# The last layer's scan: separate PSUM rings for the experts, and a scheduling priority for the scan's own work

## The chip, the cores and the metric

The kernel runs on one core of a Trainium2 chip, as one launch. The metric is the device time of one execution in microseconds; the number for a kernel is the median over its runs. The profile is one execution, recorded by the hardware profiler.

## The reference

An input of 4 sequences of 1024 tokens with 128 features passes four layers, each an attention-like part and a feed-forward part, with a residual and a layer norm after each. All is float32. What matters here is the last layer and the feed-forward part ahead of it:

```
# L2_ffn: 8 experts, the best 2 for each token (sparse)
h = silu(gate) * up;  y = h @ w2;  out = sum of the 2 chosen, weighted

# L3_attn: a selective state-space recurrence, 256 channels, 16 states
x = rmsnorm(resid); skip = x @ skip_w.T; xs = silu(conv1d(x @ in_w.T))
delta = softplus(xs @ wd1.T @ wd2.T + b); Bm = xs @ wb.T; Cm = xs @ wc.T
h[t] = exp(delta[t] * A) * h[t-1] + delta[t] * xs[t] * Bm[t]
y[t] = sum over states of h[t] * Cm[t]
out  = resid + ((y + xs * W_D) * silu(skip)) @ out_w.T

# L3_ffn: 8 experts, all computed for every token, gated by top-p 0.8
h = relu(x @ W1 + b1);  y = h @ W2 + b2;  out = sum over e of gate * y
```

## The kernel before

Every step is recorded in a Python program of generators; a scheduler then gives each engine its own list of instructions. It takes an instruction that is ready by its model of time, and among ready ones that with the lowest priority number, which is its place in the recorded program unless something else is said. On the chip each engine works its list strictly in that order, and semaphores make it wait for what it needs. Tiles come from pools; a pool of n buffers makes the writer of the next tile wait until the readers of an older one are done.

The last stage (`l3`, L1595) works on 8 halves of 512 tokens (4 sequences, 2 halves each). For each half:

- *Preparation* (`l3_prepare`, L1715): norm, transpose `pt`, input projection `pxe`, convolution and SiLU on VectorE, projection `pdb`, softplus of `pd0` and `pd1` with a chain of ScalarE and VectorE operations that keeps both in PSUM, and a write of the rows of B and C to DRAM (`rows`, L1786).
- *Scan* (`l3_scan`, L1816): 16 steps, one for each state. A step loads two broadcast rows, `bn` and `cn` (L1841, SyncE's queue, four buffers), multiplies on GpSimd (`db`, L1846), computes `da` on ScalarE (L1850) and scans on VectorE (L1851), both for two groups of 128 channels, and multiplies on GpSimd again (`hc`, L1862, four buffers). From the second sequence on an accumulating DMA adds every second `hc` to the one before (L1867). TensorE sums the `hc` in PSUM by identity products (`pys`, L1833).
- *End*: the last sums and the gate (`l3_sum`, L1876), then output product `po`, norm, transpose, router `prl` and gates `gt` (`l3_finish`, L1901).
- *Last experts* (`l3_ffn_head`, L1941, and `l3_ffn`, L1959): a head (`pgt`, `pb2`), then 8 experts, so 64 in all. An expert loads its weights `wh` (L1674, three buffers), computes four tiles `ph` (one bank each) with a ReLU on ScalarE (`hh`, L1977), one tile `py` of 16 products (one bank), and adds it to `h_acc` by four VectorE instructions (L1993).

The loop of `l3` weaves these: at each step of one half's scan it also takes one step of the end of the half before, one of the preparation of the next half, one or two of the sparse experts of the layer before (`moe`: tiles `ph` from `xgT`, `py` from `mh`, weights `wx`), and three or four of the last experts (`work`). A half's experts may begin when its end is more than three steps old (`age`).

PSUM has 8 banks of 512 float32 for each partition. During the scan `banks(y0=1, y1=1, da=2, ff=4)` (L1680) gives one bank to each sum, two to `da`, and four, as one ring `ff`, to everything else: preparation, ends, sparse experts and last experts. When all scans are recorded, `l3_experts` (L1639) closes these pools and opens one ring of eight (L1658) for what is left of the last experts.

Of the kernel before, what the change touches and what calls it, by code (L numbers as in the profile page):

```python
# [40 lines left out]
E3, NST, DDELTA, KCONV = 256, 16, 64, 4  # L41
# [17 lines left out]
class Net:  # L59
# [1535 lines left out]
    def l3(self, moe, fp):  # L1595

        c3 = self.c3  # L1600
        halves = [dict(b=b, h=h) for b in range(B) for h in range(2)]
        for i, u in enumerate(halves):
            u["prev"] = halves[i - 1] if u["h"] else None
        halves[0] = dict(self.c3["first"], **{k: halves[0][k] for k in ("prev",)})
        for i, u in enumerate(halves[1:], 1):
            u["prev"] = halves[i - 1] if u["h"] else None
        work = self.l3_experts(fp)
        end = iter(())
        for i, u in enumerate(halves):
            nxt = iter(())  # L1610
            if i + 1 < len(halves):
                if halves[i + 1]["h"] == 0:
                    while "done" not in self.m2["st"][halves[i + 1]["b"]]:
                        next(moe)
                nxt = self.l3_prepare(halves[i + 1])
            u["final"] = i + 1 == len(halves)
            for n, f in enumerate(self.l3_scan(u)):
                next(end, None)
                next(nxt, None)
                for k in range(1):  # L1620
                    next(self.m2["rest"], None)
                next(moe, None)
                if i == 0:
                    for k in range(1):
                        next(moe, None)
                for k in range(4 if n % 8 == 7 else 3):
                    next(work)
                for v in c3["todo"]:
                    v["age"] += 1
            for f in chain(end, nxt):  # L1630
                pass
            end = chain(self.l3_sum(u), self.l3_finish(u))
        for f in end:
            next(work)
        c3["all"] = True
        for f in work:
            pass

    def l3_experts(self, fp):  # L1639


        c3 = self.c3
        heads, self.wh = [], {}

        def others():

            while len(heads) < 2 and c3["todo"] and ("all" in c3 or c3["todo"][0]["age"] > 3):
                heads.append((c3["todo"].pop(0), []))
            return heads[1:]

        i = 0
        while True:
            others()
            if "all" in c3 and c3["banks"]:

                c3["banks"].close()
                c3["banks"] = None
                c3["ctx"].enter_context(self.banks(ff=8))  # L1658
            if heads:
                u = heads[0]  # L1660
                if not u[1]:
                    yield from self.l3_ffn_head(*u, fp)
                yield from self.l3_ffn(*u, i, fp, others)
                heads.pop(0)
                i += NE
            elif "all" in c3:
                return
            else:
                yield
# [6 lines left out]
    def l3_pools(self, ctx):  # L1676
        tc = self.tc
        sp = ctx.enter_context(tc.tile_pool(name="ssm", bufs=1))
        wp = ctx.enter_context(tc.tile_pool(name="ssm2", bufs=2))
        banks = ctx.enter_context(self.banks(y0=1, y1=1, da=2, ff=4))  # L1680
        self.mtags = dict(t="ff", h=("ff",), o="ff")
        self.c3.update(sp=sp, wp=wp, ctx=ctx, banks=banks)

# [257 lines left out]
    def l3_ffn_head(self, u, head, wp):  # L1941

        nc, c3, h = self.nc, self.c3, u["h"]
        ff = lambda s, n: self.psb("ff", s, n)
        acc = wp.tile([P, 4, D], F32, name="h_acc")
        head.append(acc)
        pg = ff([NE, 4, P], "pgt")
        for c in range(4):
            self.tr(pg[:, c, :], u["gt"][:, c, :])
        gT = wp.tile([NE, 4, P], F32, name="gT", bufs=1)  # L1950
        nc.scalar.copy(gT, pg)
        yield
        pb = ff([P, 4, D], "pb2")
        for c in range(4):
            self.mm(pb[:, c, :], gT[:, c, :], c3["b2"])
        nc.vector.tensor_add(acc, pb, self.xN[u["b"]][:, 4 * h : 4 * h + 4, :])
        yield

    def l3_ffn(self, u, head, i0, wp, others):  # L1959

        nc, c3, b, h, gt, acc = self.nc, self.c3, u["b"], u["h"], u["gt"], head[0]
        ff = lambda s, n: self.psb("ff", s, n)
        NK = F3 // P
        x = self.xT[b][:, h * 512 : h * 512 + 512]
        ahead = None
        for e in range(NE):
            if i0 + e == 0:
                for k in range(2):
                    self.l3_weights(k, wp)
            self.l3_weights(i0 + e + 2, wp)  # L1970
            w = self.wh.pop(i0 + e)
            hs = []
            for k in range(NK):
                ph = ff([P, 512], "ph")
                self.mm(ph, w[:, k * P : (k + 1) * P], x)
                ht = wp.tile([P, 512], F32, name="hh", bufs=6)
                nc.scalar.activation(ht, ph, AF.Relu, bias=self.col("h_b1", i=e * NK + k))  # L1977
                hs.append(ht)
                yield
            py = ff([P, 4, D], "py")  # L1980
            for c in range(4):
                for k in range(NK):
                    self.mm(
                        py[:, c, :],
                        hs[k][:, c * P : (c + 1) * P],
                        w[:, F3 + k * D : F3 + (k + 1) * D],
                        k == 0,
                        k == NK - 1,
                    )
                if c == 1:  # L1990
                    yield
            for c in range(4):
                nc.vector.scalar_tensor_tensor(  # L1993
                    acc[:, c, :],
                    py[:, c, :],
                    gt[:, c, e : e + 1],
                    acc[:, c, :],
                    ALU.mult,
                    ALU.add,
                )  # L2000
            yield

            if e >= NE - 3:
                if ahead is None and others():
                    ahead = self.l3_ffn_head(*others()[0], wp)
                if ahead is not None:
                    next(ahead, None)
        for f in ahead or ():
            pass
        self.norm(wp, acc, b, 4 * h, 4, last=True, ps=ff, act=True)  # L2010

# [193 lines left out]
```

## Time and profile before

| what | value |
|---|---|
| time, median of 3 runs | 2294.14 us (2287.42 to 2300.56) |
| profiled execution: time and span | 2289.61 us and 2287.8 us |
| TensorE busy over the span | 1974.5 us (86%) |
| VectorE, ScalarE, GpSimd busy | 1351.7 us (59%), 1207.2 us (53%), 1023.3 us (45%) |
| first product of the recurrence on GpSimd | at 1386 us |
| first `ph` of the last experts | at 1545 us |
| `po` of the last half | from 2176 us |
| GpSimd products `hc` and `db` | 128 of 2463 ns and 112 of 2593 ns in their largest groups |

In the profile's rows PE is TensorE's products, PEld its weight loads, DVE is VectorE, ACT ScalarE, POOL GpSimd, SP SyncE; a letter q behind an engine is its queue. Each row of a list of waits names the engine, tile and line that waited, then who released it, then the total in us, how often, and the longest. A float32 product of 128x128 by 512 columns is recorded as two matmul instructions. A line of the code can be that of a helper (L127 holds nearly all products), so tiles are told apart by name. Granted clock (PEclk) is the share of TensorE's full clock.

### The profile page before, as it was taken

How to read it: one execution, taken by the hardware profiler on the slowest of the kernel's cores; microseconds unless marked ns; L12 is line 12 of the kernel's file. 1: busy time of each engine (PE TensorE's matmuls, PEld its weight loads, DVE VectorE, ACT ScalarE, POOL GpSimd, SP SyncE). 2: the span in 40 equal slices, each digit the busy share in tenths (PEclk: the TensorE clock that was granted, in tenths of full speed). 3: DMA queues.
4: the chain of work that ended last, by engine and by line, in shares of the span. 5: the costliest groups of instructions: out<-in, count | busy, mean ns of one | idle time of the engine just before them, and what ended most of it. 6: DMA issues, size and time to landing. Idle time of an engine off the chain costs nothing.

```text
span 2287.8 us, 46393 instructions
## 1 busy us (share of the span) xinstructions
PE 1974.5 (86%) x17806; PEld 1382.2 (60%) x17806; DVE 1351.7 (59%) x3693; ACT 1207.2 (53%) x2621; POOL 1023.3 (45%) x812
## 2 busy tenths in 40 slices
PE   6667979879999999999989876589888989898998
PEld 3455655444477777787767664346555656565666
DVE  7457743424355565665555556686777787877521
ACT  6543443332244444444555456476767786767443
POOL 5100230000023235224243429988789979888500
PEclk9757989979999999999999987799999999999999
DMA  3000110005000010031223147456776666676421
GB/s 107 0 15 23 30 39 1 19 10 174 1 3 2 3 35 15 17 91 46 76 70 88 32 142 231 127 182 196 202 204 178 177 169 192 175 208 178 122 60 51
DMA packets 138558, 211.10 MB, mean 92 GB/s; under 512 B 18597, under 2 KB 75936, under 8 KB 137952
## 3 DMA queue, kind: packets, MB, share of 16 engines
q1 hardware_dynamic: 126192, 173.87, 24.7%
q0 software_dynamic: 12144, 34.26, 7.1%
q8 instruction: 140, 2.29, 0.4%
q14 instruction: 82, 0.67, 0.1%
HBM read 160.29 MB, written 23.16 MB: 80 GB/s over the span
## 4 chain that ended last, share of the span: by engine, by line
PE 40%; DVE 13%; ACT 11%; issue 4%; DMA 2%; POOL 1%; SPq 0%; ACTq 0%; DVEq 0%; POOLq 0%
PE py L127 7%; PE ph L127 6%; PE po L1126 5%; DVE db L1851 5%; PE pqk L127 4%; PE pa_m L127 4%; PE kp_mo L127 3%; PE pr L1196 2%; PE pv L127 2%; PE pys L127 2%; ACT hh L1977 2%; ACT da L1850 1%; PE pt L131 1%; PE kp_mo L131 1%; ACT xN L174 1%
## 5 line engine op out<-in xcount | busy, mean ns | idle before, releaser
L1059 POOL TENSOR_TENSOR qt<-r_q,sb_c_turn 128x256 f32<-128x256 f32 (+1 forms) x256 | 164.0, 661 | 448.5 <-ACT r_q L1051 442.9
L1862 POOL TENSOR_TENSOR hc<-db,cn 128x1024 f32<-128x1024 f32 x128 | 312.9, 2463 | 63.5 <-PE pys L127 27.1
L127 PEld LDWEIGHTS py<-wh,hh 128*128 128x128 f32 x2048 | 248.6, 193 | 85.6 <-issue 36.1
L1846 POOL TENSOR_TENSOR db<-ud,bn 128x1024 f32<-128x1024 f32 x112 | 284.1, 2593 | 12.7 <-DMA wh<-in_wH 6.2
L127 PE MATMUL py<-wh,hh 128*128 128x128 f32 x2048 | 257.1, 278 | 22.9 <-ACT hh L1977 12.5
L127 PE MATMUL ph<-xT,wh 128*128 128x512 f32 x512 | 250.3, 606 | 16.8 <-ACT hh L1977 5.9
L1977 ACT ACTIVATE hh<-ph,sb_cols 128x512 f32<-128x512 f32 x256 | 170.6, 681 | 131.9 <-PE ph L127 105.5
L1117 DVE TENSOR_TENSOR a<-pa_m,sb_c_near 128x256 f32<-128x256 f32 x256 | 96.7, 420 | 202.6 <-PE pa_m L127 202.6
L1074 ACT ACTIVATE kN<-kp_mo,sb_c_trig 128x128 f32<-128x128 f32 x448 | 130.2, 372 | 132.0 <-PE kp_mo L131 122.2
L1850 ACT ACTIVATE da<-dl,aneg 128x512 f32<-128x512 f32 x224 | 153.1, 689 | 77.8 <-DVE db L1851 76.6
L127 PE MATMUL pys<-hc,sb_c_ident 128*128 128x512 f32 x324 | 159.7, 621 | 29.3 <-POOL hc L1862 21.3
L1851 DVE TENSOR_TENSOR_SCAN db<-da,carry,db 128x512 f32<-128x512 f32 x128 | 158.0, 1268 | 21.1 <-POOL db L1846 11.9
L1851 DVE TENSOR_TENSOR_SCAN db<-da,db 128x512 f32<-128x512 f32 x128 | 149.6, 1207 | 9.5 <-POOL db L1846 6.0
L127 PEld LDWEIGHTS ph<-xT,wh 128*128 128x128 f32 x512 | 89.8, 194 | 98.1 <-issue 57.1
L1993 DVE SCALAR_TENSOR_TENSOR h_acc<-py,gt,h_acc 128x128 f32<-128x128 f32 x256 | 71.8, 343 | 124.6 <-PE py L127 124.0
L127 PE MATMUL pqk<-xT,wE 128*128 128x256 f32 x512 | 136.8, 390 | 8.2 <-ACT coT L1193 4.2
L127 PEld LDWEIGHTS pys<-hc,sb_c_ident 128*128 128x128 f32 x324 | 61.0, 199 | 96.7 <-issue 60.6
L729 POOL DMA_INDIRECT orows<-o,ix x20 | 18.9, 944 | 186.6 <-DVE o L727 160.4
L127 PEld LDWEIGHTS pqk<-xT,wE 128*128 128x128 f32 x512 | 89.0, 194 | 22.0 <-DVE cv L1036 8.1
L131 PE MATMUL pt<-sb_c_ident,xN 128*128 128x128 f32 x224 | 54.4, 343 | 51.4 <-ACT xN L174 32.2
L1193 ACT COPY coT<-pt 128x512 f32<-128x512 f32 x64 | 37.6, 587 | 116.1 <-PE pt L131 116.1
L127 PE MATMUL po<-ht,wD 128*128 128x512 f32 x192 | 94.3, 598 | 0.0
(456 smaller groups left out, 4340.2 us busy)
## 6 DMA issues: line engine op xcount, KB each, us to landing
wx<-in_wF SPq DMA_DIRECT2D x92, 384.0 KB, 3.3
bn<-rows SPq DMA_DIRECT2D x128, 256.0 KB, 5.0
cn<-rows SPq DMA_DIRECT2D x128, 256.0 KB, 4.3
wh<-in_wH SPq DMA_DIRECT2D x64, 512.0 KB, 4.1
hc<-hc POOLq DMA_DIRECT2D x47, 512.0 KB, 6.6
xrows<-zero SPq DMA_DIRECT2D x4, 1472.0 KB, 11.9
xg<-xrows SPq DMA_DIRECT2D x20, 256.0 KB, 3.0
yrows<-ys SPq DMA_DIRECT2D x20, 256.0 KB, 3.3
```

The costliest lines, as they stand in the source:

```text
L127: return self.nc.tensor.matmul(out=out, lhsT=lhsT, rhs=rhs, start=start, stop=stop)
L131: self.nc.tensor.transpose(out, in_, self.ident[0:n, 0:n])
L1059: nc.gpsimd.tensor_mul(u["qt"][:, m, a:], u["q"][:, a:], c2["turn"][:, m, o + a : o + 2 * P])
L1074: self.nc.scalar.activation(u["kN"][:, c, m, :], pk[:, c, :], AF.Copy, scale=trig[:, k, m : m + 1])
L1117: nc.vector.tensor_mul(u["a"][:, i, :, :], pa[i], self.c2["near"][:, None, :].to_broadcast([P, 2, P]),)
L1126: self.nc.tensor.matmul(out=u["po"][self.HALF[j], i, c, :], lhsT=lhsT, rhs=rhs, start=key not in u["begun"], stop=True, skip_group_check=True,
L1846: nc.gpsimd.tensor_mul(db, ud, bc[0])
L1850: nc.scalar.activation(da, dl[:, ec, :], AF.Exp, scale=aneg[:, j : j + 1])
L1851: nc.vector.tensor_tensor_scan(db[:, ec, :], da, db[:, ec, :], carry[:, ec, n : n + 1] if h else 0.0, ALU.mult, ALU.add,)
L1862: nc.gpsimd.tensor_mul(hc, db, bc[1])
L1977: nc.scalar.activation(ht, ph, AF.Relu, bias=self.col("h_b1", i=e * NK + k))
L1993: nc.vector.scalar_tensor_tensor(acc[:, c, :], py[:, c, :], gt[:, c, e : e + 1], acc[:, c, :], ALU.mult, ALU.add,)
```

## The change

It has three parts.

1. The ring `ff` of four banks becomes two rings of two during the scan: `ff` for preparation, ends and sparse experts, `ex` for the last experts and their heads. The last norm of an expert's half keeps `ff`.
2. When all scans are recorded, the ring of eight becomes `ff=2, ex=6`.
3. One step of the scan, one of the end of the half before and one of the preparation of the next are recorded inside `high_priority(offset=1000)`: in the scheduler they count as if recorded 1000 instructions earlier. Sparse experts and last experts keep their place. A scan's generator is now stepped 16 times by a counter, and is run out (it has nothing left to record) ahead of the rest of the end and the preparation, which stand outside of the priority.

```diff
             u["final"] = i + 1 == len(halves)
-            for n, f in enumerate(self.l3_scan(u)):
-                next(end, None)
-                next(nxt, None)
+            scan = self.l3_scan(u)
+            for n in range(NST):
+                with self.tc.high_priority(offset=1000):
+                    next(scan)
+                    next(end, None)
+                    next(nxt, None)
                 for k in range(1):
                     next(self.m2["rest"], None)
                 next(moe, None)
...
-            for f in chain(end, nxt):
+            for f in chain(scan, end, nxt):
                 pass
             end = chain(self.l3_sum(u), self.l3_finish(u))
...
-                c3["ctx"].enter_context(self.banks(ff=8))
+                c3["ctx"].enter_context(self.banks(ff=2, ex=6))
...
-        banks = ctx.enter_context(self.banks(y0=1, y1=1, da=2, ff=4))
+        banks = ctx.enter_context(self.banks(y0=1, y1=1, da=2, ff=2, ex=2))
         self.mtags = dict(t="ff", h=("ff",), o="ff")
...
     def l3_ffn_head(self, u, head, wp):
-        ff = lambda s, n: self.psb("ff", s, n)
+        ff = lambda s, n: self.psb("ex", s, n)
...
     def l3_ffn(self, u, head, i0, wp, others):
-        ff = lambda s, n: self.psb("ff", s, n)
+        ff = lambda s, n: self.psb("ex", s, n)
...
-        self.norm(wp, acc, b, 4 * h, 4, last=True, ps=ff, act=True)
+        self.norm(wp, acc, b, 4 * h, 4, last=True, ps=self.bank("ff"), act=True)
```

The built program of the changed kernel has the same instructions of work on every engine; ScalarE's table loads are 112 instead of 110. What differs is their order from about the first sparse experts beside the recurrence on.

## The prediction

> **What bounds the kernel now.** The change touches only the last stage, so I first asked the table of stretches for its three phases: the recurrence alone, the recurrence with the last experts beside it, the last experts alone.
>
> ```profile
> core 0: us, PE busy (x) PEld busy (x) DVE busy (x) ACT busy (x) POOL busy (x), PEclk, DMA share, GB/s
> 1380.00:1540.00 160.00, 110.83 (x416) 66.15 (x417) 117.74 (x185) 96.11 (x200) 150.44 (x75) 0.84 0.54 169
> 1540.00:2150.00 610.00, 551.04 (x2752) 361.55 (x2751) 455.22 (x871) 436.94 (x792) 529.55 (x276) 0.98 0.68 187
> 2150.00:2288.00 138.00, 123.32 (x688) 88.14 (x686) 33.40 (x120) 56.52 (x92) 0.00 (x0) 0.97 0.19 56
> ```
>
> Up to 1540 us POOL is the limit: 150.4 of 160 us busy with the recurrence's products. From there on TensorE (PE) is: 551 of 610 us beside the recurrence, 123 of 138 after it, and its work is the same before and after the change. So the end moves by what PE's idle time changes, and there are 610 - 551 = 59 us of it between 1540 and 2150. POOL has 80 us free there. The list of waits says what PE idles for (engine and line that waited, releaser: total us, times, longest):
>
> ```profile
> PE py L127 <- ACT hh L1977: 12.4, 15, 1.8
> PE pys L127 <- DMA hc<-hc: 7.8, 4, 3.0
> PE ph L127 <- ACT hh L1977: 6.8, 5, 2.9
> ...
> PE psk L127 <- ACT hh L1977: 3.7, 3, 2.2
> ...
> PE ph L127 <- DVE h_acc L1993: 2.2, 3, 1.0
> ```
>
> The four rows with hh or h_acc are waits for an expert's activation or for a PSUM bank: 12.4 + 6.8 + 3.7 + 2.2 = 25 us. The other 34 us are spread over sums of the recurrence, preparation, norms and the sparse experts. The same list for POOL shows what the priority could free:
>
> ```profile
> POOL hc L1862 <- PE pys L127: 27.1, 11, 9.1
> POOL hc L1862 <- DVE db L1851: 10.1, 7, 3.3
> ```
>
> Last, the timeline of experts alone, with eight banks (start, duration, engine, line, out<-in; in brackets the idle time before):
>
> ```profile
> 2254.44 1.13 DVE L1993 SCALAR_TENSOR_TENSOR h_acc<-py,gt,h_acc 128x128 f32<-128x128 f32 x4 [5.88 <-PE py L127]
> ...
> 2254.68 3.60 PE L127 MATMUL ph<-xT,wh 128*128 128x512 f32 x8
> ...
> 2255.80 0.69 ACT L1977 ACTIVATE hh<-ph,sb_cols 128x512 f32<-128x512 f32 x1 [0.71 <-PE ph L127]
> ...
> 2258.12 3.73 PE L127 MATMUL py<-wh,hh 128*128 128x128 f32 x32
> ...
> 2261.69 3.60 PE L127 MATMUL ph<-xT,wh 128*128 128x512 f32 x8
> ```
>
> An expert is four ph (8 instructions, 2254.68 to 2258.12, so 0.86 us each) and one py (32 instructions, 3.57 us): 7.01 us, back to back, because the ph of one expert stand ahead of the py of the expert before.
>
> **The change, part by part.** All counts of order below are from the built program of the changed kernel: where its instructions stand on each engine.
>
> *Two rings of two.* Experts are numbered from 1 to 64. With two banks a ph needs the bank of the ph two before it, and the second ph of an expert needs the bank of the last py. Built, no ph of experts 9 to 48 stands ahead of the end of the previous py (before: 28 of 160 do). What such an expert costs when ACT and VectorE (DVE) are free, from the timeline: h_acc ends at 2255.57, 0.89 us after the first ph starts. An activation ends 0.95 us after its ph's slot (0.26 until 2255.80, then 0.69). For the hand-over back to PE I take 0.06 us, from a relu of 0.67 us that starts at 1979.82 and the ph that it releases at 1980.55. First ph 0 to 0.86; second 0.95 to 1.81 (lost 0.09); third waits for the first's activation, 1.87 to 2.73 (0.06); fourth 2.82 to 3.68 (0.09); py starts at 3.74 (0.06), runs three products (0.33) and stands until the fourth activation at 4.69 (0.62); 3.24 us more end it at 7.93. That is **0.92 us lost per expert**.
>
> - Experts 49 to 56 run after the recurrence and before the new pools: 8 x 0.92 = **+7 us**.
> - Experts 1 to 48 run beside it. The gap inside py: 30 of 40 experts (9 to 48) have nothing else there, so 48 x 0.75 x 0.62 = 22 us. The gap before the second ph: 28 of 40 have other work in it, mostly sums of 1.72 us, which hide it. The other 30%, 14 experts, meet a DVE that is 75% busy (455 of 610) with scans of 1.2 us; an h_acc behind one is 0.75 x 1.2 = 0.9 us late: 14 x 1.0 = 14 us. The three gaps before third ph, fourth ph and py are open in about 105 of 144 cases; ACT is 72% busy with operations of 0.69 us, a delay of 0.5 us, and 105 x 0.57 = 60 us. After one such stall the next activation is no longer late, so I take half, 30. Sum 66 us, against the 25 us of such waits today: **+41 us**. Upper end, no halving: +71. Lower end, the isolation from the recurrence's long holds saves more than two banks cost: -10.
>
> Against that stands what the other ring gains: preparation (pd0 and pd1 hold two banks together) no longer takes banks from experts, but the sparse experts, preparation and ends now share two.
>
> *Priority.* Compared at equal numbers of finished experts, scans on DVE stand 0 to 10 instructions of 256 further forward from expert 30 on; around the ninth they even stand back by 8. When the last half's output product (po) is issued, 195 of 256 ph have been issued instead of 206: 2.75 experts, 2.75 x 7.01 = 19 us of PE work, go behind the recurrence. That by itself costs nothing if PE is never idle. What it can save are PE's 34 us of other waits, of which some 15 hang on the recurrence's own chain (7.8 for the accumulating DMA, then db, dl and gT copies): **-15 us**, ends 0 and -33. POOL's 27.1 us behind pys may go too; but POOL has 80 us free, so this starts the ends earlier and not the experts' end. What is late next is each expert's activation: on ACT the da of the next steps stand ahead of hh, and a da waits for a scan (53.5 us, 56 times, in the list).
>
> *Queues.* On SP the bn and cn loads move ahead of the sparse experts' weights (at the start 8 of them, 256 KB each, before two of 384 KB); each lands in 3 to 5 us and four buffers cover it. SP now stands 194.5 us in weight loads (wh) that wait for a py to free their buffer, and the bn and cn loads behind them with it; slower experts lengthen that. POOL's 80 us hide it, so zero; 10 us if that cover is gone. On POOL the row gathers of batch 1 (8 DMA issues, 7.5 us together by the 0.94 us of the row for L729) move about ten products back; they feed the next batch's preparation, hidden by the same spare time.
>
> *A hole between experts 8 and 9.* Built, preparation, router, head (pgt, pb2) and sparse experts of the second half stand together on PE there, with no expert to fill, where before only pgt, pb2 and one sum did. The work is not new, the waits in its chain are: between 0 and 15 us, taken as **+5** (its nearest row is the 6.8 us for ph behind hh).
>
> *Eight banks in the end, six now.* An expert alone holds at most five; zero, and 0.92 a piece for the last eight (+7) if that is wrong.
>
> Sum: 7 + 41 - 15 + 5 = **+38 us**. The profiled execution took 2289.6 us (span 2287.8 and 1.8 around it), 4.5 under the median of the runs, 2294.1 (2287.4 to 2300.6). Forecast 2289.6 + 38 = **2328 us**. Ends: 7 - 10 - 33 + 0 = -36, so 2254; 7 + 71 + 0 + 15 = +93, so 2383.
>
> A rule weighs against the change here. The rows first: the granted clock was 0.84 in the stretch with PE 69% busy and 0.97 to 0.98 at about 90%. The Trainium skill, page "TensorE: Matmul & The Clock Gate", section "A second HAM failure mode: psum-queue depth-cycling", tells of a kernel whose small pauses between matmul groups, from cycling through PSUM banks, made the clock gate swing. By that rule the stretch of 551 us would run at 0.84: 551 x (0.98 / 0.84 - 1) = 92 us more. By the rows an expert of 7.93 us is 88% busy, as today's last stretch is (89%, 0.97), and nothing is added; I go by the rows.
>
> **Rivals.**
>
> 1. *Faster: the recurrence stops stalling and PE follows.* Place: POOL's 27.1 + 10.1 us behind pys and db, and the 34 us of PE's other waits. If the ring costs no more than it isolates, half of PE's 59 us goes: 2289.6 - 30 + 7 = 2267. For it: POOL is the second busiest engine (87%), and 28 of 40 of the second gaps have work in them. Against: PE is the bound, and the 0.62 us inside py is open in 30 of 40. It decides once the ring's cost (experts 1 to 48, those after, the hole) stays below the waits that the priority removes: with all 33 removed, below +21 for the first term.
> 2. *No change.* PE's work is the same, the order at equal experts differs by a few scans, and what the ring loses the priority gives back: 2294.
> 3. *Slower by far.* ACT and DVE serve recurrence first, every expert is late at every bank, and the hole is whole: the upper ends, 2375.
> 4. *It does not do what it says.* The lead of at most 10 scans is five steps of about 5 us; then only the ring acts: 7 + 41 + 5, 2343. That lies inside the forecast's own range.
>
> **How the numbers follow.** Forecast with rival 4: 0.47 (2306 to 2355). Rival 3: 0.15. Rival 2: 0.13. Rival 1: 0.25 (2250 to 2282). A measurement of this kernel can tell about 0.5%, 11.5 us, from no change, so slower has 0.62, same 0.13, faster 0.25. The range reaches to 2262 below and 2383 above.
>
> **What would show it.** Right: PE's waits for hh and h_acc between first expert and last scan rise from 25 us to about 65; the cadence of experts 49 to 56 is near 7.9 us; the last po comes at about 2190 (now 2176) with 15.25 experts behind it; POOL's idle time grows. Wrong: PE's idle time in that stretch stays under 59 us, or the last po comes before 2157, 19 us earlier, with experts at 7.0 us behind it; then rival 1 holds. A granted clock well under 0.97 would make both wrong.

## The result and the profile after

The changed kernel takes **2379.34 us** (median of 4 runs, 2377.19 to 2382.98) where the kernel before takes 2290.78 (4 runs): ratio 1.0385, 95% interval 1.0358 to 1.0411. The forecast said 38 us more; it is 88. The sign was right and the time lies inside the range, but the forecast's size is less than half of what was measured, and one term had the wrong sign. The profiled execution took 2382.98 us (span 2381.2), 93.4 more than that of before (2289.61).

The table of stretches of the kernel before, cut finer than in the prediction, and then the same for the changed kernel. The number behind each x counts instructions, so matmuls done can be compared at equal times:

```profile
core 0: us, PE busy (x) PEld busy (x) DVE busy (x) ACT busy (x) POOL busy (x), PEclk, DMA share, GB/s
1540.00:1675.00 135.00, 118.40 (x630) 81.10 (x629) 95.60 (x184) 96.78 (x202) 111.56 (x62) 0.97 0.69 201
1675.00:1725.00 50.00, 45.00 (x232) 30.82 (x232) 35.52 (x68) 29.23 (x51) 41.75 (x23) 0.93 0.76 207
1725.00:2150.00 425.00, 387.63 (x1893) 249.63 (x1892) 324.10 (x619) 310.94 (x542) 376.25 (x193) 0.99 0.67 181
```

```profile
1540.00:1675.00 135.00, 118.36 (x608) 79.93 (x608) 96.71 (x179) 86.42 (x171) 115.91 (x64) 0.96 0.67 192
1675.00:1725.00 50.00, 38.95 (x147) 24.31 (x148) 26.54 (x61) 30.74 (x59) 12.16 (x7) 0.73 0.43 120
1725.00:2150.00 425.00, 368.02 (x1704) 234.57 (x1703) 308.96 (x584) 298.16 (x528) 363.76 (x188) 0.96 0.66 176
2150.00:2243.00 93.00, 83.98 (x397) 52.09 (x396) 47.99 (x99) 44.89 (x70) 48.66 (x25) 0.98 0.45 118
2243.00:2381.00 138.00, 122.02 (x664) 84.48 (x662) 29.42 (x113) 52.19 (x82) 0.00 (x0) 0.96 0.19 55
```

By 2150 us PE has done 22 + 85 + 189 = 296 matmuls fewer. At 0.205 us each (387.63 / 1893, before) that is 61 us of work put off: 5 us in the first stretch, 17 in the 50 us from 1675, 39 in the 425 us that follow. (Another 76 matmuls were missing already at 1540 us.) So work is put off in a single place and, more of it, all along the recurrence.

The single place is on POOL. Its timeline (start, duration, line, out<-in; in brackets the idle time before):

```profile
1674.07 2.35 POOL L1865 TENSOR_TENSOR hc<-db,cn 128x1024 f32<-128x1024 f32 x1 [1.25 <-DVE pmv L159]
1676.35 1.76 POOL L1870 DMA_DIRECT2D hc<-hc  x2
1715.95 9.28 POOL L1849 TENSOR_TENSOR db<-ud,bn 128x1024 f32<-128x1024 f32 x4 [37.84 <-DVE ud L1813]
```

and PE's timeline in that hole:

```profile
1672.25 1.02 PE L127 MATMUL pxe<-xnT,sb_s_in 128*128 128x512 f32 x2
1677.62 2.05 PE L127 MATMUL ph<-xgT,wx 128*128 128x128 f32 x8 [4.35 <-issue]
1682.17 1.22 PE L127 MATMUL py<-wx,mh 128*128 128x128 f32 x4 [2.50 <-DVE xs L1780]
...
1698.54 1.16 PE L127 MATMUL ph<-xgT,wx 128*128 128x128 f32 x8 [0.78 <-ACT db L1788]
1701.73 0.68 PE L127 MATMUL py<-wx,mh 128*128 128x128 f32 x4 [2.04 <-DVE gt L1939]
...
1708.01 5.49 PE L127 MATMUL ph<-xT,wh 128*128 128x512 f32 x6
```

The recurrence of the next half can't start, because its preparation (`xs`, `db`, at last `ud`) goes through in single file with the end of the half before (`prl`, `gt`) and the sparse experts (`xgT`, `mh`), and the last experts have nothing to put between: no tile from `wh` runs from 1671 to 1708. PE waits in pieces of 1 to 4 us, its clock falls to 0.73, and when an expert comes, its first three ph take 5.49 us where they need 2.58.

The lists of waits of the changed kernel, PE's and then POOL's (1540 to 2250 us):

```profile
PE py L127 <- ACT hh L1980: 22.7, 18, 4.4
PE ph L127 <- ACT hh L1980: 14.0, 15, 3.8
PE ph L127 <- DVE h_acc L1996: 9.4, 12, 2.4
```

```profile
POOL db L1849 <- DVE ud L1813: 40.7, 2, 37.8
POOL hc L1865 <- PE pys L127: 25.7, 9, 7.5
POOL hc L1865 <- DVE db L1854: 17.5, 9, 7.4
```

PE's rows for an expert's tiles sum to 46 us, up from 25. Seen alone that is 21 us of 93, and here is a trap. The timeline of experts that run alone after the recurrence shows what the list leaves out:

```profile
2267.84 1.02 PE L127 MATMUL ph<-xT,wh 128*128 128x512 f32 x2
2269.23 3.09 PE L127 MATMUL ph<-xT,wh 128*128 128x512 f32 x6 [0.36 <-DVE h_acc L1996]
2272.15 4.11 PE L127 MATMUL py<-wh,hh 128*128 128x128 f32 x32
2276.10 1.02 PE L127 MATMUL ph<-xT,wh 128*128 128x512 f32 x2
```

An expert comes every 8.26 us (2267.84 to 2276.10) instead of 7.01, at a granted clock of 1.00 in this stretch: 1.25 us lost, of which only 0.36 is recorded as a wait. Starts tell the rest: first ph 1.39 us where 0.86 is needed, the other three 2.92 for 2.58, py 3.95 for 3.57. Stops of a few tenths are swallowed by the modelled ends and counted as busy. That, a lower clock and 76 matmuls more that were left at 1540 us are why PE's busy time from 1540 on grew by 57 us (674.36 to 731.33).

### The profile page after: what moved, and what is told of

Its sections match the earlier page's. It is cut to its first block, busy times and chain, and to the rows that moved or that the text cites. A ratio compares the mean times of both kernels' runs of the same rounds, so it can differ in the third digit from the quotient of the medians.

```text
span 2381.2 us, 46369 instructions
## 1 busy us (share of the span) xinstructions
PE 2031.4 (85%) x17806; PEld 1406.4 (59%) x17806; DVE 1354.5 (57%) x3693; ACT 1214.7 (51%) x2623; POOL 1024.4 (43%) x812
## 4 chain that ended last, share of the span: by engine, by line
PE 42%; DVE 14%; ACT 11%; issue 3%; POOL 2%; DMA 1%; SPq 0%; ACTq 0%; POOLq 0%; DVEq 0%
PE py L127 8%; PE ph L127 6%; PE po L1126 5%; DVE db L1854 5%; PE pqk L127 4%; PE pa_m L127 4%; PE kp_mo L127 2%; PE pys L127 2%; PE pv L127 2%; PE pr L1196 2%; ACT hh L1980 2%; ACT da L1853 2%; PE pt L131 1%; DVE h_acc L1996 1%; PE kp_mo L131 1%
## 5 line engine op out<-in xcount | busy, mean ns | idle before, releaser
L1865 POOL TENSOR_TENSOR hc<-db,cn 128x1024 f32<-128x1024 f32 x128 | 309.6, 2445 | 80.5 <-PE pys L127 25.7
L127 PEld LDWEIGHTS py<-wh,hh 128*128 128x128 f32 x2048 | 255.2, 199 | 77.7 <-ACT hh L1980 50.4
L127 PE MATMUL ph<-xT,wh 128*128 128x512 f32 x512 | 268.0, 631 | 30.2 <-ACT hh L1980 14.0
L127 PE MATMUL py<-wh,hh 128*128 128x128 f32 x2048 | 265.6, 284 | 25.5 <-ACT hh L1980 24.0
```

The lines of the kernel that those rows point to most:

```text
L127: return self.nc.tensor.matmul(out=out, lhsT=lhsT, rhs=rhs, start=start, stop=stop)
L1865: nc.gpsimd.tensor_mul(hc, db, bc[1])
```

## The experiments

Each run stands beside runs of the kernel before on the same chip. In two groups of runs that kernel took 2331 and 2325 us instead of 2287 to 2291, so ratios are compared below, not times.

**The parts alone.** Rings apart without the priority; priority without the rings; the last pools without either.

```diff
 # split_only, against the changed kernel
-                with self.tc.high_priority(offset=1000):
-                    next(scan)
-                    next(end, None)
-                    next(nxt, None)
+                next(scan)
+                next(end, None)
+                next(nxt, None)
 # prio_only, against the kernel before
+                with self.tc.high_priority(offset=1000):
+                    next(scan)
+                    next(end, None)
+                    next(nxt, None)
 # tail_only, against the kernel before (experts use ex from here on)
-                c3["ctx"].enter_context(self.banks(ff=8))
+                c3["ctx"].enter_context(self.banks(ff=2, ex=6))
```

> The changed kernel without the priority: two rings of two banks (ff=2, ex=2), then ff=2, ex=6; scans, preparation and ends in their recorded place. Theory A (the experts' ring of two banks costs most of the 88 us): 2350 to 2395 us. Theory B (the priority costs most: it puts the recurrence's ScalarE and VectorE work ahead of every expert's activation and h_acc): 2295 to 2330 us. Theory C (ends and preparation are the ones that suffer in their ring of two banks, with or without the priority): as A, but with the recurrence ending late and few waits of ph for hh.

Measured: 2360.46 us, 1.0314 (1.0274 to 1.0353).

> The kernel before with the priority of 1000 alone, one ring of four banks and eight in the end. Theory A: 2270 to 2305 us, as the priority alone moves little or saves some of the 34 us of other waits. Theory B: 2330 to 2380 us, with waits of py and ph for hh well above 25 us. If the two parts only hurt together, this and the split alone both stay under 2320.

Measured: 2286.77 us, 0.998 (0.9958 to 1.0002).

> The kernel before with only the pools of the end changed (ff=2, ex=6 in place of eight in one ring; the last norms use ff). All theories: 2288 to 2300 us. Were six banks too few in the end, 2295 to 2310 us: at most 1 us for each of the last eight experts.

Measured: 2287.63 us, 0.9996 (0.9975 to 1.0016).

The split alone costs 72 us (2360.46 - 2288.40), the priority alone nothing, the last pools nothing. The priority on top of the split adds 0.7% (1.0385 against 1.0314), some 16 us; by the intervals of the two ratios it is between 5 and 27.

The profiled executions tell where. Three points cut them: the last `co` (VectorE, L1171, the stage ahead of this one), the first `ph` of the last experts, and the last `po`.

| us, one trace each | before | prio_only | split_only | changed |
|---|---|---|---|---|
| last `co` to first `ph` of the last experts | 213.0 | 216.4 | 224.3 | 224.2 |
| from there to the last `po` | 633.3 | 627.9 | 665.5 | 683.5 |
| from there to the end | 109.8 | 110.6 | 137.7 | 137.5 |

With the split 122 instead of 100 instructions of `ph` stand behind the last `po`, so 2.75 experts more, 19 us of work at 7.01 each. The middle stretch, though it holds that much less, is 32 us longer: 51 us lost there. 11 us are lost ahead of it and some 9 behind it. (tail_only, which costs nothing, gives 212.9, 634.3 and 111.1, so the stretches repeat within a few us.) The priority adds its 18 us in the middle stretch alone.

**Which ring is short.** A bank is taken from `da` and given to one ring, to the other, or to none; the changed kernel otherwise.

```diff
-        banks(y0=1, y1=1, da=2, ff=2, ex=2)
+        banks(y0=1, y1=1, da=1, ff=2, ex=3)    # after_ex3
+        banks(y0=1, y1=1, da=1, ff=3, ex=2)    # after_ff3
+        banks(y0=1, y1=1, da=1, ff=2, ex=2)    # after_da1
```

> The changed kernel with one bank moved from da to the experts' ring (da=1, ff=2, ex=3). Theory A: the waits of ph and py for a bank mostly go, 2310 to 2345 us, less what a single da bank costs the scans. Theory B: 2370 to 2400 us, since hh is late whatever the number of banks. Theory C: 2375 to 2400 us, the other ring is as it was and da is worse.

Measured: 2348.04 us, 1.0269 (1.0222 to 1.0316).

> The changed kernel with one da bank and one PSUM bank left unused (da=1, ff=2, ex=2): the base for the two kernels that give this bank to a ring. If a second da bank matters, 2385 to 2420 us; if not, 2375 to 2385.

Measured: 2395.11 us, 1.0455 (1.04 to 1.0509).

> The changed kernel with the da bank given to the other ring (da=1, ff=3, ex=2). Theory A (the experts' ring is what is short): within 15 us of the kernel that leaves the bank unused, and well above the 2348 us of ex=3. Theory C (preparation, ends and sparse experts are short): 2320 to 2350 us, as good as ex=3 or better.

Measured: 2364.53 us, 1.032 (1.0267 to 1.0373).

Against after_da1 a third bank is worth some 43 us (by the ratios) in the experts' ring or 31 us in the other: both are short, and after_ff3 lies between the two theories. In after_ff3 POOL's list has no row any more for `db` behind `ud` or `dl`, and `db` sat idle for 0.0 us on its page: with a third bank for preparation and sparse experts the hole is gone. But the gain lies elsewhere: the first `ph` of the last experts comes 209.5 us after the last `co` (237.8 in after_da1), and from there to the last `po` it takes 684.2 us (683.9). So closing the hole is not seen to gain anything in the stretch where it stood.

**Is PE free where it waits?** Six products more for each expert, ahead of py, into the same bank; py overwrites them.

```diff
             py = ff([P, 4, D], "py")
+            for k in 2 * (0, 1, 2):
+                self.mm(py[:, 0, :], hs[k][:, 0:P], w[:, F3 + k * D : F3 + (k + 1) * D])
```

> The split without priority, with six more products in each expert ahead of py: the first three products of py, twice, overwritten by the real ones (0.64 us of added TensorE work per expert at full clock, 41 us in all; the output is the same). They stand in the gap in which py waits for the fourth activation. If this gap is open as worked out (0.62 us) and TensorE loses clock by such pauses: 2330 to 2355 us, with a granted clock above 0.95 in the recurrence (0.94 without). If the gap is open and the clock doesn't follow it: 2355 to 2370. If the gap is mostly filled by other work already: 2380 to 2400.

The price in that expectation is half of the true one: a float32 product is two instructions, so an expert gets 12 of them (3.57 / 32 = 0.112 us each), 1.34 us, 86 us in all. Measured: 2433.24 us, 1.0618 (1.0561 to 1.0674), some 70 us above split_only by the ratios. Only some 16 of the 86 us fell into idle time, and the intervals leave room for 0 to 32. Alone, experts of this kernel come every 9.22 us, as its timeline shows:

```profile
2304.08 1.02 PE L127 MATMUL ph<-xT,wh 128*128 128x512 f32 x2
...
2313.30 1.02 PE L127 MATMUL ph<-xT,wh 128*128 128x512 f32 x2
```

0.97 us more than 8.25, so 0.37 us of an expert's gap stood at this place.

**Are the experts late because the recurrence is served first?** The priority is given to the experts' steps instead, on the split rings and on the shared one.

```diff
                 for k in range(4 if n % 8 == 7 else 3):
-                    next(work)
+                    with self.tc.high_priority(offset=1000):
+                        next(work)
```

> The split, with the last experts (in place of scans, preparation and ends) recorded 1000 instructions ahead. If the experts lose their time by late activations and h_acc behind the recurrence's work on ScalarE and VectorE: 2310 to 2340 us. If it is the chain inside an expert itself (0.92 us and the clock), whatever stands ahead: 2350 to 2370. If the recurrence is then held up and sets the end: over 2375.

Measured: 2381.76 us, 1.0392 (1.0335 to 1.0448).

> The kernel before with the priority of 1000 instructions given to the experts' steps in place of the recurrence's, on the shared ring of four. Theory (the order of instructions matters only where a ring is short): within 10 us of the kernel before, 2278 to 2298. Rival 1 (PE's waits for hh are activations that stand behind the recurrence's on ACT, so experts first saves most of the 25 us): 2265 to 2275. Rival 2 (experts first starve the recurrence, as in split_xprio with +21): 2300 to 2315.

Measured: 2340.15 us beside 2331.22, 1.0021 (0.9992 to 1.005).

Neither gains. On split rings both priorities came out 0.7 to 0.8% above split_only, the experts' one with an interval that overlaps it; on the shared ring neither shows a change.

**Splitting, or fewer banks?** The kernel before with three shared banks; with one `da` and five; with one `da` and four.

```diff
-        banks(y0=1, y1=1, da=2, ff=4)
+        banks(y0=1, y1=1, da=2, ff=3)    # shared_ff3, a bank unused
+        banks(y0=1, y1=1, da=1, ff=5)    # da1_ff5
+        banks(y0=1, y1=1, da=1, ff=4)    # da1_ff4, a bank unused
```

> The kernel before with three shared banks in place of four, the fourth left unused; no priority, no rings apart. Theory (what costs is the splitting: any user that is held up blocks only itself in a shared ring, but with two banks apart a user waits while the other ring's bank stands empty): three shared banks cost less than two rings of two, so under half of split_only's +72, 2295 to 2322. Rival (an expert simply needs more banks, however they are shared; three shared are worse than two and two): 2360 or more.

Measured: 1.0365 (1.0313 to 1.0417). My theory of that moment fell: three in one ring lose as much as two and two. POOL's list for this kernel shows the same wait for preparation, in more pieces:

```profile
POOL db L1846 <- DVE ud L1810: 48.5, 3, 22.3
POOL hc L1862 <- DVE db L1851: 31.5, 21, 3.7
POOL hc L1862 <- PE pys L127: 30.1, 9, 5.1
POOL db L1846 <- ACT dl L1811: 18.0, 2, 14.9
```

Yet with only an expert or two to serve, its three banks run at full pace (py's second part starts 7.01 us after the one before):

```profile
2303.99 3.06 PE L127 MATMUL py<-wh,hh 128*128 128x128 f32 x26
...
2311.00 3.06 PE L127 MATMUL py<-wh,hh 128*128 128x128 f32 x26
```

So the pace of an expert alone does not tell what a ring costs in company.

> The kernel before with one bank for da and five shared, no priority: the same eight banks as after_ex3 (2348) and after_ff3 (2365), but not split. Theory (splitting is the cost): the second da bank was worth some 16 us in the changed kernel (2395 against 2379), and a fifth shared bank gives back little, so 2285 to 2305, some 50 us below after_ex3. Rival (the count of banks that experts hold is the cost): as after_ex3 without the priority's 19, about 2329, since experts held about three of five. If the fifth bank helps more than the second da bank, it is faster than the kernel before: 2270 to 2285.

Measured: 1.0045 (1.002 to 1.007).

> The kernel before with one bank for da and four shared, one bank unused: the unsplit twin of after_da1 (2395). Theory (splitting): 2288 + 16 = 2304, so the split with its priority costs 91 at seven banks, as it costs 91 at eight. Rival (the changed kernel loses at da, since its priority makes the da banks the bound): then da1_ff4 is within 5 us of the kernel before and the whole 16 us belongs to the changed kernel.

Measured: 1.0107 (1.006 to 1.0155).

Both as the theory had it. Five shared banks lose 0.45% where the same five, split three and two in after_ex3 and after_ff3, lose 2.7 and 3.2%; four shared lose 1.1% where two and two in after_da1 lose 4.6% (one `da` bank in all of these). The split ones have the priority, 0.7%, besides. The steep step is from three shared to four, 3.7% (with two `da` banks); a fifth is worth some 0.6% (with one).

**Can the split be mended by moving users between the rings?** py of an expert from the other ring (without and with the priority, and with the `da` bank given to that ring); sparse experts in the experts' ring.

```diff
-            py = ff([P, 4, D], "py")
+            py = self.psb("ff" if c3["banks"] else "ex", [P, 4, D], "py")   # split_pyff, after_pyff
+        banks(y0=1, y1=1, da=1, ff=3, ex=2)                                 # pyff_ff3, besides
+        self.mtags = dict(t="ex", h=("ex",), o="ex")                        # split_moex
```

> split_only (1.031 of before) with one tile moved: an expert's py takes its bank from the ring ff that preparation, ends and sparse experts use, until the last pools; the two ex banks hold only ph (and the head's pgt and pb2). Built, 85 of the 160 ph of experts 9 to 48 then stand ahead of the end of the previous py; none do in split_only. Theory (a ring of two that holds ph and py in turn makes an expert serial: 8.25 us in the traces, where 7.01 is possible, at a clock of 1.00; 1.24 x 56 = 69 us): most of the loss goes although the number of banks is the same, ratio 1.00 to 1.012, and the experts after the recurrence come every 7.0 to 7.3 us. Rival (the shortage of banks as such, since three shared banks lose as much, with a serial part of 7.01 us): ff is now shorter still, so ratio 1.03 or more.

Measured: 1.0369 (1.0307 to 1.043).

> The changed kernel (1.0385) with the same one tile moved, so with the priority. Theory (serial experts): as split_pyff, with the priority's share on top, 1.00 to 1.02. Rival (shortage): 1.035 or more. If the priority costs only where experts are serial, it is within 0.4% of split_pyff; if it costs by itself at split rings, it is 0.8% above.

Measured: 1.0377 (1.0315 to 1.0438).

The serial expert is not the whole cause: its ph now stand ahead of the last py, and nothing is gained. The loss moved: PE's waits for `hh` and `h_acc` fall from 47 us in split_only to 28 in split_pyff (from 1540 us on), and POOL's for `ud` and `dl` rise to 57 us in split_pyff and 77 in after_pyff.

> split_pyff with a bank moved from da to ff: one da, three ff (with py), two ex (ph). Compare da1_ff5, the same banks in one ring (1.0045), and da1_ff4 (1.011). Theory (it matters who shares, not that rings are apart): 1.00 to 1.012. Rival (any split costs): 1.02 or more.

Measured: 1.0271 (1.0211 to 1.0331), the rival's side: three and two lose 2.3% against five shared.

> split_only (1.0314) with the sparse experts' tiles moved from the ring ff to the ring ex, so that preparation and ends have their two banks for themselves. Every kernel whose preparation shares a ring of two shows one long hole on POOL, 35 to 38 us in which the recurrence waits for the next half's dl or ud, and PE has no expert to run; after_ff3, with three banks there, shows none. Theory (the hole is the sparse experts and preparation taking turns at two banks): POOL's waits for dl and ud fall from 37 us to under 10 and PE gains some 15 to 25 us, ratio 1.020 to 1.025. Rival (the hole goes, but experts now wait for the sparse experts' banks): no hole and 1.030 or more. Third (the hole is the preparation's own chain): hole stays, 1.030 or more.

Measured: 1.0386 (1.0354 to 1.0419), the rival's side again. The lists of POOL in split_only and then in split_moex:

```profile
POOL hc L1864 <- PE pys L127: 36.1, 12, 7.6
POOL db L1848 <- ACT dl L1813: 35.0, 1, 35.0
```

```profile
POOL hc L1864 <- DVE db L1853: 41.5, 17, 5.8
POOL hc L1864 <- PE pys L127: 19.0, 8, 3.6
```

The 35 us hole is there without any priority, so the priority did not make it. Nor does it take two rings: POOL stood 66 us for `ud` and `dl` with three shared banks. Without the sparse experts in that ring it is gone, and the time is 0.7% above split_only's, not below it. PE now waits 10.1 us for sparse experts in the experts' ring (ph behind `ys`), which fits; that this is all of it is not shown.

**Which part of the priority costs on split rings?** On the scans alone, and on the preparation alone.

```diff
                 with self.tc.high_priority(offset=1000):
                     next(scan)
-                    next(end, None)
-                    next(nxt, None)
+                next(end, None)
+                next(nxt, None)          # scan_prio; nxt_prio: only next(nxt, None) inside
```

> The changed kernel with the priority on the scans alone; the steps of preparation and of the ends have none. Theory (the priority's 19 us on split rings come from the preparation that is brought forward as a block, with POOL held up 38 us and PE's clock lowered): as split_only, ratio 1.029 to 1.033. Rival (scans ahead of the experts' activations and sums cost it): as the changed kernel, 1.036 to 1.041.

Measured: 1.0314 (1.0246 to 1.0382).

> The changed kernel with the priority on the preparation's steps alone; scans and ends have none. scan_prio, with the scans alone, came out at split_only's ratio (1.0314, interval 1.0246 to 1.0382) and leaves preparation and ends for the priority's further 0.7% on split rings. Theory (preparation brought forward as a block): 1.036 to 1.041. Rival (it takes scans and preparation together, or the ends): 1.029 to 1.034.

Measured: 1.0357 (1.033 to 1.0383).

The first agrees with no cost, but its interval reaches to the changed kernel; the second lies between both theories. From the first expert to the last `po` their traces take 670 and 669 us, split_only's 666 and the changed kernel's 684, so neither part alone brings the priority's 18 us; single traces, the first from a group of runs where all was slower, settle no more, and this stays open. The hole is in both (35.6 and 33.0 us), so it is not what tells them apart. No version beat the kernel before clear of noise.

## Why the prediction was right in sign and wrong in size

- **PE's work is the same, its idle time decides**: right, 17806 matmuls in both.
- **One expert alone, 0.92 us**: measured 1.25. Two errors half cancel. The gap inside py was worked out with three products as 0.33 us; they are six instructions, 0.67, so the gap is 0.28 and not 0.62, and split_fill found 0.37 there. The gap before the second ph, forecast as 0.09, is 0.53: `h_acc` ends 1.34 us after the first ph starts (2268.05 + 1.13 - 2267.84), not 0.89. I had taken that from the old order, where other work stands between. Experts 49 to 56 cost some +9 (the last row of the table less 19) or, by 8 x 1.25, +10, not +7.
- **Experts 1 to 48, +41, and the hole, +5**: near in sum, and in part by luck. The split lost 51 us between the first expert and the last po where the two terms said 46. But the pieces of the 41 are not shown: the gap inside py, a third of the 66 us, was taken at twice its size, and with py in the other ring, where experts are less serial, the loss stayed. What the term did not hold is who else loses. Whatever was moved between the rings, in three divisions of four banks (1.031 to 1.039), the loss stayed, and it is as large as that of one bank fewer in a shared ring (1.0365). Its lower end counted isolation as a gain, and no run shows one. Four shared banks served users that do not all need them at once; that a bank now stands idle in one ring while the other waits fits all of these runs, but was not recorded directly.
- **The hole by itself**: the built order had rightly shown that the second half's preparation stands there without an expert. Its waits were priced by a row of 6.8 us, when POOL stood for 38. By the matmuls done at equal times it put off 17 us of work, above the upper end of 15; but after_ff3, without it, is no faster in that stretch, so what it costs in the end is not shown.
- **Sparse experts, preparation and ends on two banks**: named and costed at nothing. They cost 11 us before any of the last experts has started (224 us from the last `co` against 213), and nothing there with a third bank (209.5).
- **The waits to watch, 25 to about 65 us**: 46. The list under-reports, as the 0.36 of 1.25 shows; the time lost was larger than the list forecast, not smaller. POOL's idle time from 1540 to 2150 grew, as forecast, from 80 to 118 us.
- **Priority, -15: the step that failed.** The term took it that PE's waits on the recurrence's own chain would be saved once that chain stood further forward. It measured +16 on the split rings and -2, which is nothing, on the shared one: 31 of the 50 us that the forecast was short. The rows of the term, in the kernel before and then in prio_only (1540 to 2250 us; the first row of before stands in the prediction, 7.8):

```profile
PE pb L127 <- ACT gT L1951: 3.7, 4, 1.7
...
PE py L127 <- ACT db L1785: 2.2, 1, 2.2
...
PE ph L127 <- ACT dl L1811: 1.4, 1, 1.4
...
PE pgt L131 <- ACT dl L1811: 0.7, 1, 0.7
```

```profile
PE pys L127 <- DMA hc<-hc: 3.8, 4, 2.0
PE pb L127 <- ACT gT L1954: 3.5, 3, 1.4
...
PE ph L127 <- ACT db L1788: 2.0, 1, 2.0
...
PE py L127 <- ACT db L1788: 0.6, 1, 0.6
```

They sum to 15.8 us before, 9.9 in prio_only, 9.0 in split_only and 8.0 in the changed kernel. So with the rings apart there was 1 us of them left for the priority, and on the shared ring the 6 us it took did not show in the time. POOL's 27.1 us behind pys became 25.7 in the changed kernel and 22.1 in prio_only. Why it costs 16 us on split rings is open. The forecast's own row for what is late next (da ahead of hh on ACT) was named and not charged, but PE's waits for `hh` and `h_acc` are 47 us in split_only and 46 with the priority, and the experts' priority costs as much (1.0392).
- **Queues, 0, and the last pools, 0**: right. POOL waits 5.2 us for a `cn` row and 2.7 for a `bn` row in the whole stage, and tail_only changes nothing.
- **Last po at about 2190 with 15.25 experts behind**: the 15.25 are right, and the +28 us behind it are the 2.75 experts and the slower eight. But it ends at 2243.7, 66 us after that of the kernel before (2178.0), where the forecast had 14: what was missed lies ahead of it.
- **The clock, nothing by the rows**: half right. Experts with regular stops of 0.36 us ran at 1.00. Where waits were longer the clock was lower: 0.73 in the hole, 0.96 against 0.99 in the long stretch, 0.94 against 0.98 from 1540 to 2150 us. Weighted by busy time that is 38.95 x (1 - 0.73 / 0.93) = 8 and 368.02 x (1 - 0.96 / 0.99) = 11, an estimate of some 20 us. The rule of the Trainium skill ("TensorE: Matmul & The Clock Gate", "A second HAM failure mode: psum-queue depth-cycling") had the direction; the 92 us that I drew from it were more than four times too many.
- **Rival 3, slower by far, 2375**: nearest in number, but not by its terms. It had the priority at nothing, the experts at +71 and the hole at +15. (The prediction gives its lower end as 2254 by the sum and as 2262 with the chances; nothing rests on that.)

Sum by the runs: 72 for the split with its hole (53 forecast), nothing for the last pools (0), 16 for the priority on top of it (-15): 88, where 88 were measured and 38 forecast. By the traces' stretches it is 11 ahead of the first expert (0 forecast), 51 up to the last po (46), 9 behind it (7) and 18 for the priority (-15), 89 in all.

## What to carry to other kernels

A shared ring of buffers is a reserve; before dividing it, price every user of each part, not only the one that the change is for, and compare with the shared ring that has one buffer fewer. Take lost time from the starts of equal work (here 8.26 us against 7.01), since the list of waits holds only part of it. Before counting on a priority for one chain, see whether the bound engine's waits for that chain are worth anything in time: here the shared ring gave up 6 of 16 us of them, and the time did not follow.

## What the hardware showed besides

A long wait costs more than its length. In the changed kernel the second part of py, 26 instructions, takes 3.17 us after a short wait and 4.52 after one of 4.42 us:

```profile
2000.79 4.52 PE L127 MATMUL py<-wh,hh 128*128 128x128 f32 x26 [4.42 <-ACT hh L1980]
...
2012.10 3.17 PE L127 MATMUL py<-wh,hh 128*128 128x128 f32 x26 [0.87 <-ACT hh L1980]
```

That is 1.35 us lost behind the wait, about a third of it again. In the traces of all the kernels here, from 1540 us on, 97 such pieces of 26 instructions stand behind a recorded wait of up to 1.3 us, and 92 of them took 3.17 us; all 9 behind a wait of 2.5 us or more took 4.52 to 5.72; between these waits it is 9 of 26 that took longer than 4. Filling the gaps did not buy this back: with the added products of split_fill the clock beside the recurrence rose from 0.94 to 0.96, but of their own 86 us the kernel paid some 70.
